# Transposes off TensorE: layer 2's input turned by VectorE and transfers, the RMS factor spread through DRAM, bias rows added on VectorE

## The chip, the core and the metric

The kernel runs on one core of one Trainium2 chip. Five engines work side by side, each through its own list of instructions in order: TensorE (PE in the profile; PEld is its loading of weights), VectorE (DVE), ScalarE (ACT), GpSimd (POOL) and SyncE (SP), which here only issues transfers (DMA). They meet through semaphores. The metric is the device time of one execution in microseconds; the median of three executions of the kernel before is 2365.2 us (2365.17 to 2367.01).

## The reference

32 graphs of 512 nodes with 256 features each go through four graph layers. Everything is float32. Cut to what matters (weights and small constants left out):

```python
def _layernorm(x):                      # over the last axis
    return (x - mean(x)) / sqrt(var(x) + 1e-5)

# layer 0
h = (1 + eps) * x + adj @ x
x = _layernorm(x + (relu(h @ W1 + b1) @ W2 + b2))                  # 256 -> 512 -> 256
# layer 1
h = adj @ (x @ W.T + b)
x = _layernorm(x + where(h > 0, h, alpha * h))
# layer 2
h = layer_norm(x, gamma, beta)
x = _layernorm(x + (x + relu((adj @ h) @ W_rel + b_rel + h @ W_root)))
# layer 3
h = (epsilon * x + adj @ x) @ W1 + b1                              # 256 -> 1024
h = silu(h * rsqrt(mean(h * h) + 1e-6) * rms_weight)               # RMS over the 1024
x = _layernorm(x + (h @ W2 + b2))                                  # 1024 -> 256
```

## The kernel before

A graph's features lie in a tile `room` of 128 partitions by 1024 floats: 128 nodes of each of four chunks, 256 features per chunk. Matrix products are done by a scheme with seven block products for a 2x2 split where eight are usual (`seven`, `left_sums`, `right_sums`); VectorE makes the sums of blocks that this needs, and adds results from PSUM. A product of 256 columns or of 128 is one matmul; in the trace each appears twice, as two passes.

No engine's order is written out by hand. Each step (`plan.do`, `plan.move`) is recorded as an `Op` with the engines that can do it and an estimated duration. `Plan.order` then runs through time and at each point gives the engine that is free first the operation with the lowest rank, where the rank grows with the number of the graph (`RULES`: period, pace, last, near). Up to `FLIGHT` = 4 graphs are in work at once, limited by 36 rooms, 12 small tiles (`few`) and the 8 banks of PSUM. Transfers are all issued by SP, in order, at most 8 at a time; the planner counts 0.45 us per issue and a fixed part before and after the data. It also keeps GpSimd's sums and VectorE's sums of two SBUF operands apart in time (`port`). All instructions pass through one helper, so almost every row of the profile has the line L266 (transfers: L280); tiles tell them apart.

Five places matter for what follows.

- `layer2` (L935 to L953). The product `h @ W_root` needs `h` with features on partitions. L938 to L943 turn it: for each of two feature blocks four transposes on TensorE (`flip`, a matmul with the identity `ident`) fill one bank, and one `copy` brings the bank to `hT`. `dense_sums` (L950) then makes VectorE's sums of `hT` and the aggregate `aT`, and `dense_add` multiplies.
- `layer3` (L955 to L990). `squares` sums the squares of the 1024 features, `column_sums` (L793) reduces over partitions with a transposing reduction and small sums, `inv_sqrt` has GpSimd raise to the power -0.5 with the result on 128 partitions, and L975 to L977 spread the 512 factors over all partitions with four flips into one bank `pr`. L981 multiplies the hidden features by `pr` on VectorE.
- `plus_row` (L874) adds the bias row of layers 0 and 3 to the residual, as four sums of 256 columns on GpSimd each time, eight per graph.
- `Adjacency` (L634). The adjacency arrives in four transfers of 256 KB. Layers 0 and 3 need it with a multiple of the identity added, layers 1 and 2 without. `sums` saves the four diagonal blocks in a room by transfers within SBUF (`carry`, L659 to L665), `with_loops` adds, `restore` (L667) carries them back.
- the order of layers per graph: `layer0`, `layer1`, `layer2`, `layer3`, with the output transfer at the end of `layer3` (L990).

```python
        for j in range(DC):
            ps = bank(N)
            for c in range(NC):
                flip(ps[:, c * P : (c + 1) * P], h[:, c, j * P : (j + 1) * P])
            copy(hT.chunk(j), ps)
```

Of the kernel before, what the change touches and what calls it, by code (L numbers as in the profile page):

```python
# [10 lines left out]
F32 = mybir.dt.float32  # L11
# [3 lines left out]
P = 128  # L15
# [11 lines left out]


def in_psum(x):
    return isinstance(x, Part) and x.room.pool.psum  # L30
# [35 lines left out]
def gpsimd_time(n):  # L66
    return 0.15 + n * 0.0024, 0.05


def power_time(n):  # L70
    return 0.37 + n * 0.158, 0.04
# [4 lines left out]
ISSUE, ADVANCE, AFTER, LANES = 0.45, 1.5, 0.35, 8  # L76
# [18 lines left out]
RULES = [(50, 2, last, near) for last in (12, 20) for near in (0, 0.5, 1)]  # L95


class Pool:


    def __init__(self, tiles, grain, spare, psum):
        self.tiles, self.grain, self.spare, self.psum = tiles, grain, spare, psum
        self.clear()

    def clear(self):
        self.rooms = [None] * len(self.tiles)

    def free(self):

        return sorted(  # L110
            (0.0 if r is None else r.until, i)
            for i, r in enumerate(self.rooms)
            if r is None or not r.left
        )


class Room:


    def __init__(self, pool):  # L120
        self.pool = pool
        self.uses = 0
        self.clear()

    def clear(self):
        self.index = None
        self.left = self.uses
        self.until = 0.0


class Part:
# [34 lines left out]
    def place(self):  # L166
        v = self.room.pool.tiles[self.room.index]
        for step in self.steps:
            v = step(v)
        return v  # L170
# [3 lines left out]
class Op:  # L174

    graph: int
    rank: tuple
    ways: dict  # L180
    port: set
    yields: bool
    kbytes: float
    rooms: list = field(default_factory=list)
# [6 lines left out]
class Plan:  # L191
# [10 lines left out]
    def grains(self, x):  # L202
        part = isinstance(x, Part)
# [4 lines left out]
        for step, n in dims[:-1]:  # L208
            starts = [s + step * i for s in starts for i in range(n)] if step else starts
        step, n = dims[-1]  # L210
        return {
            (key, g)
            for s in starts
            for g in range(s // grain, (s + step * (n - 1)) // grain + 1)
        }

    def add(self, ways, out, ins, ordered=None, port=(), kbytes=0):
        me = len(self.ops)
        op = Op(self.graph, (self.graph, me), ways, port, "scalar" in ways, kbytes)
        self.ops.append(op)  # L220
        before, results = set(), set()
        writes = self.grains(out) if out is not None else set()
# [22 lines left out]
    def do(self, out, *ways, ordered=None, scrap=None):  # L245
# [3 lines left out]
        port = set()  # L249
        for e, method, _, args, kw in ways:  # L250
            tiles = [x for x in (*args, *kw.values()) if isinstance(x, (bass.AP, Part))]
            ins += tiles
            if e == "gpsimd" and kw.get("op") != ALU.pow or e == "vector" and not (
                method.startswith("bn_") or any(in_psum(x) for x in tiles)
            ):
                port.add(e)

        def issue(engine, method, args, kw):
# [14 lines left out]
            out, ins, ordered, port,  # L273
        )

    def move(self, out, src, kbytes, inward=True):


        def issue():
            self.nc.sync.dma_start(*(x.place() if isinstance(x, Part) else x for x in (out, src)))  # L280

        self.add(
            {"sync": ((ISSUE, ADVANCE + wire_time(kbytes) + AFTER), issue)},
            out if inward else None, [src] if isinstance(src, Part) else [], kbytes=kbytes,
        )
# [31 lines left out]
    def order(self, period, pace, last, near):  # L317
# [15 lines left out]
        oldest, port, wire, lanes = 0, 0.0, 0.0, [0.0] * LANES  # L333
        can_start = {i for i, n in enumerate(behind) if not n}
        done = []
        while can_start:
# [4 lines left out]
            def rooms_free(op):  # L341

                count = {}
                for r in op.rooms:
                    if r.index is None:
                        count[r.pool] = count.get(r.pool, 0) + 1
                at = 0.0
                for pool, n in count.items():
                    if pool not in room_at:
                        room_at[pool] = pool.free()  # L350
                    n += pool.spare[min(op.graph - oldest, len(pool.spare) - 1)]
                    if op.graph - oldest >= self.flight or n > len(room_at[pool]):
                        return None
                    at = max(at, room_at[pool][n - 1][0])
# [3 lines left out]
            for i in can_start:  # L358
# [4 lines left out]
                if op.kbytes:  # L363
                    wait = max(wait, lanes[0])
                at = {
                    e: max(free[e], wait, ready[i][e], port if e in op.port else 0.0)
                    for e in op.ways
                }
                way = min(at, key=lambda e: at[e] + sum(op.ways[e][0]) + (YIELD if op.yields and e == "vector" else 0.0))
# [11 lines left out]
            if op.kbytes:  # L381
                wire = max(wire, t + ADVANCE) + wire_time(op.kbytes)
                end = wire + AFTER
                lanes = [*lanes[1:], end]
            if engine in op.port:
                port = end
            for r in op.rooms:
                if r.index is None:
                    r.index = r.pool.free()[0][1]
                    r.pool.rooms[r.index] = r  # L390
# [16 lines left out]
def tile_gnn_stack(ctx: ExitStack, tc: tile.TileContext, a: dict, out: bass.AP):  # L407
# [36 lines left out]
    FLIGHT, ROOMS, SMALL = 4, 36, 12  # L444
# [3 lines left out]
    psum = ctx.enter_context(tc.tile_pool(name="psum", bufs=1, space=bass.MemoryType.PSUM))  # L448
    plan = Plan(nc, FLIGHT)

    def pool(kind, name, n, size, grain, spare):
        return Pool(
            [kind.tile([P, size], F32, tag=f"{name}{i}", name=f"{name}{i}") for i in range(n)],
            grain, spare, kind is psum,
# [3 lines left out]
    rooms = pool(work, "room", ROOMS, NC * D, P, (0, 4, 6, 8))  # L458
# [5 lines left out]

    def gpsimd(method, n, *args, **kw):
        return "gpsimd", method, gpsimd_time(n), args, kw
# [22 lines left out]
    def both(method, o, x, y, engines):  # L489
        plan.do(o, *(e(method, span(o), x, y) for e in engines))  # L490

    def add(o, x, y, *engines):
        both("tensor_add", o, x, y, engines or (vector,))

    def sub(o, x, y, *engines):
# [590 lines left out]
```

## Time and profile before

| | |
|---|---|
| median of three executions | 2365.2 us |
| the profiled execution | 2366.0 us |
| its span (first to last instruction) | 2364.2 us |
| granted TensorE clock, mean | 0.997 |
| TensorE matmuls with `ident`, from `room` (layer 2) | 256, 273 ns each |
| the same from `few` (the RMS factor) | 128, 274 ns each |
| GpSimd bias rows, 128x256 | 256, 194.6 us busy, 769 ns each |
| GpSimd powers, 128x4 and 128x8 | 160, 212.5 us busy |
| VectorE sums of two SBUF operands, 128x512 | 672, 464.2 us busy, 696 ns each |
| VectorE sums of SBUF and PSUM, 128x512 (`room<-room,ps`) | 256, 170.5 us busy, 679 ns each |
| transfers within SBUF, 128 KB | 252, 2.2 us to landing |
| adjacency transfers, 256 KB | 128, 5.0 us to landing |
| output transfers, 512 KB | 32, 3.0 us to landing |

The page that these come from is of one execution. Busy time is the time in which at least one instruction of an engine was under way; [...]two of them overlap, and the distance between two starts is shorter than the duration. A group's row names output and inputs, shape and count, then busy time, the mean duration, and the idle time of the engine just before. Transfers are listed with the time from issue to landing; what SP spends on the issue itself is a separate record.

### The profile page before, as it was taken

What the parts mean: (1) busy time and instruction counts of PE and PEld (TensorE: products, weight loads), DVE (VectorE), ACT (ScalarE), POOL (GpSimd) and SP (SyncE); (2) the same over time, 40 slices, a digit from 0 to 9 for tenths busy, and PEclk for the clock granted to TensorE, in tenths of its full rate; (3) what the DMA queues carried; (4) which work ended last, traced back from release to release, by engine and by line L of the source; (5) the groups of instructions that cost most, each with busy time, mean ns of one, the idle gap of its engine ahead of it and who ended that gap; (6) DMA issues with size and microseconds to landing.
All of it is one profiled execution on the core that took longest, in us unless ns stands there. A gap on an engine that the chain in (4) does not pass through costs nothing.

```text
span 2364.2 us, 40948 instructions
## 1 busy us (share of the span) xinstructions
PE 2330.0 (99%) x14362; PEld 2135.4 (90%) x14362; DVE 2138.4 (90%) x5485; ACT 1570.1 (66%) x3994; POOL 407.7 (17%) x422
## 2 busy tenths in 40 slices
PE   8999999999999999999999999999999999989997
PEld 7899989999999999999999999999999989978997
DVE  6899989999999999999999999999999999988997
ACT  3767666667666676766676666776666766565764
POOL 1112111111121121111111211111111112111111
PEclk9999999999999999999999999999999999999999
DMA  7001110111110111101111101111011111011000
GB/s 218 12 8 54 50 54 12 52 50 51 53 35 30 50 54 50 54 14 50 50 52 52 44 20 50 54 50 54 14 50 50 52 52 46 23 52 48 10 10 28
DMA packets 103487, 107.25 MB, mean 45 GB/s; under 512 B 10865, under 2 KB 78193, under 8 KB 103281
## 3 DMA queue, kind: packets, MB, share of 16 engines
q1 hardware_dynamic: 103280, 104.64, 14.5%
q8 instruction: 113, 1.85, 0.3%
q14 instruction: 94, 0.76, 0.1%
HBM read 54.80 MB, written 16.78 MB: 30 GB/s over the span
## 4 chain that ended last, share of the span: by engine, by line
PE 91%; DVE 4%; DMA 2%; ACT 1%; issue 1%; SPq 0%; POOL 0%; POOLq 0%; ACTq 0%; DVEq 0%
PE ps L266 91%; DVE room L266 3%; ACT room L266 1%; DVE few L266 1%; DMA room<-in_x_dram 1%; ACT scrap L266 1%; DMA room<-room 1%; SPq L280 0%; DMA L_gnn_eps<-in_L_gnn_eps_dram 0%; DMA room<-in_adj_dram 0%; POOL few L266 0%; ACT L266 0%; POOLq L1082 0%; DVE L_gnn_W L266 0%; DVE A L266 0%
## 5 line engine op out<-in xcount | busy, mean ns | idle before, releaser
L266 PE MATMUL ps<-room,room 128*128 128x256 f32 x3584 | 911.9, 380 | 9.8 <-DMA room<-in_x_dram 5.8
L266 DVE TENSOR_TENSOR room<-ps,room 128x256 f32<-128x256 f32 (+1 forms) x1344 | 629.6, 475 | 149.3 <-PE ps L266 122.6
L266 PEld LDWEIGHTS ps<-room,room 128*128 128x128 f32 x3584 | 650.1, 191 | 88.8 <-issue 7.1
L266 DVE TENSOR_TENSOR room<-room,room 128x512 f32<-128x512 f32 (+1 forms) x1120 | 640.6, 585 | 9.9 <-ACT room L266 3.1
L266 PE MATMUL ps<-L_gnn_W,room 128*128 128x128 f32 (+1 forms) x3584 | 622.7, 291 | 7.2 <-ACT room L266 4.9
L266 PEld LDWEIGHTS ps<-L_gnn_W,room 128*128 128x128 f32 x3584 | 525.3, 192 | 31.1 <-ACT room L266 7.2
L266 PE MATMUL ps<-A,room 128*128 128x128 f32 x3072 | 489.2, 276 | 1.8 <-ACT room L266 1.1
L266 PEld LDWEIGHTS ps<-A,room 128*128 128x128 f32 x3072 | 434.8, 192 | 15.8 <-ACT room L266 1.3
L266 PE MATMUL ps<-room,L_gnn_W 128*128 128x256 f32 x1536 | 424.6, 380 | 1.0 <-DVE room L266 0.9
L266 ACT ACTIVATE room<-ps,L_gnn_b_c 128x256 f32<-128x256 f32 x768 | 318.2, 472 | 157.2 <-PE ps L266 157.0
L266 POOL TENSOR_TENSOR few<-few,mhalf 128x4 f32<-128x4 f32 (+1 forms) x160 | 212.5, 1329 | 1211.0 <-DVE few L266 1208.5
L266 ACT ACTIVATE room<-ps 128x256 f32<-128x256 f32 (+1 forms) x546 | 215.0, 407 | 298.5 <-PE ps L266 294.7
L266 ACT ACTIVATE room<-room,few 128x256 f32<-128x256 f32 x624 | 341.0, 603 | 107.0 <-DVE few L266 103.7
L266 DVE TENSOR_TENSOR room<-room 128x256 f32<-128x256 f32 (+1 forms) x640 | 330.4, 518 | 18.0 <-DMA room<-in_adj_dram 5.7
L266 POOL TENSOR_TENSOR room<-room,L_gnn_b 128x256 f32<-128x256 f32 x256 | 194.6, 769 | 739.6 <-PE ps L266 519.0
L266 PE MATMUL ps<-room,A 128*128 128x256 f32 x1152 | 319.2, 380 | 3.0 <-ACT room L266 3.0
L266 PEld LDWEIGHTS ps<-room,L_gnn_W 128*128 128x128 f32 x1536 | 279.7, 191 | 33.1 <-DVE room L266 2.2
L266 ACT ACTIVATE room<-room 128x1024 f32<-128x1024 f32 (+2 forms) x260 | 245.8, 946 | 18.1 <-DVE room L266 16.5
L266 ACT ACTIVATE room<-room,L_gnn_rms_weight_c 128x512 f32<-128x512 f32 x256 | 179.7, 718 | 111.3 <-DVE room L266 108.2
L266 PEld LDWEIGHTS ps<-room,A 128*128 128x128 f32 x1152 | 206.5, 191 | 27.1 <-ACT room L266 4.2
L266 ACT ACTIVATE scrap<-room 128x256 f32<-128x256 f32 x384 | 157.2, 411 | 74.3 <-DVE room L266 63.1
L266 ACT ACTIVATE scrap<-room,few 128x256 f32<-128x256 f32 x384 | 190.7, 498 | 18.1 <-DVE few L266 16.3
(53 smaller groups left out, 1453.4 us busy)
## 6 DMA issues: line engine op xcount, KB each, us to landing
room<-in_adj_dram SPq DMA_DIRECT2D x128, 256.0 KB, 5.0
room<-room SPq DMA_DIRECT2D x252, 128.0 KB, 2.2
room<-in_x_dram SPq DMA_DIRECT2D x32, 512.0 KB, 6.0
out_dram<-room SPq DMA_DIRECT2D x32, 512.0 KB, 3.0
L_gnn_W<-in_L_gnn_W_dram SPq DMA_DIRECT2D x2, 1024.0 KB, 8.5
L_gnn_W<-in_L_gnn_W_dram SPq DMA_DIRECT2D x2, 512.0 KB, 8.1
L_gnn_b<-in_L_gnn_b_dram SPq DMA_DIRECT2D x3, 128.0 KB, 5.0
L_gnn_W_rel<-in_L_gnn_W_rel_dram SPq DMA_DIRECT2D x1, 256.0 KB, 7.2
```

The costliest lines, as they stand in the source:

```text
L266: getattr(getattr(self.nc, engine), method)(to, *(put(x) for x in args), **kw)
```

## The change

For all graphs but the first and the last (`alone()`), the twelve flips per graph are replaced. `turned` has VectorE transpose the 32x32 blocks of `h` (two instructions of 128x512 into a room `squares`), and 16 transfers of 32 partitions by 8 pieces of 32 floats (128 bytes) each put the blocks in their places in `hT`. `everywhere` gathers the RMS factors in a 32x32 square with four small copies, transposes it on VectorE, writes 16 rows of 128 bytes to a line in DRAM, and reads the line back to all 128 partitions; `pr` is then a tile in SBUF. The bias rows become two sums of 128x512 on VectorE each. The diagonal blocks are no longer kept in SBUF: two of them are read again from the input in DRAM (as four transfers of 64 KB), two are saved to DRAM and read back (graph 0 keeps the old way). `with_loops` adds in place.

The planner changes with it: five graphs in work, rooms that can be taken in halves (`short`), dependencies followed by groups of 32 partitions, no keeping apart of GpSimd and VectorE, other rules of rank, other estimates for the power (0.3 + 0.21 per column for 0.37 + 0.158) and for the time after a transfer (0.8 us for 0.35), other reserves of free rooms, 11 small tiles for 12. The order of all engines is thus new.

The core of the diff; bookkeeping of half rooms and renamed helpers are left out:

```diff
-    return 0.37 + n * 0.158, 0.04
+    return 0.3 + n * 0.21, 0.04
...
-ISSUE, ADVANCE, AFTER, LANES = 0.45, 1.5, 0.35, 8
+ISSUE, ADVANCE, AFTER, LANES = dict(sync=0.45, gpsimd=1.5), 1.5, 0.8, 8
...
-RULES = [(50, 2, last, near) for last in (12, 20) for near in (0, 0.5, 1)]
+RULES = [(p, c, last, near) for p, c in ((36, 2), (45, 2.5)) for last in (12, 20) for near in (0.25, 0.5)]
...
-    FLIGHT, ROOMS, SMALL = 4, 36, 12
+    FLIGHT, ROOMS, SMALL = 5, 36, 11
...
+    memory = ctx.enter_context(tc.tile_pool(name="memory", bufs=1, space=bass.MemoryType.DRAM))
     plan = Plan(nc, FLIGHT)
+    lines = cycle([memory.tile([N], F32, tag=f"line{i}", name=f"line{i}") for i in range(FLIGHT)])
+    diagonals = cycle(
+        [
+            memory.tile([P, 2, 2, P], F32, tag=f"diagonal{i}", name=f"diagonal{i}")
+            for i in range(FLIGHT)
+        ]
+    )
+    def alone():
+        return plan.graph in (0, B - 1)
...
-    rooms = pool(work, "room", ROOMS, NC * D, P, (0, 4, 6, 8))
+    rooms = pool(work, "room", ROOMS, NC * D, P, (0, 2, 4, 4))
...
-            kept = room(4, HC, P)
-            self.plain = [kept[:, i] for i in range(4)]
-            for d, o in zip(self.plain, self.loops):
-                if plan.graph:
-                    carry(d, o)
+            if plan.graph:
+                self.kept = next(diagonals)
+                for i in (2, 3):
+                    d = self.kept[:, i - 2]
+                    name = f"{self.kept.tensor.name}{i}"
+                    plan.move(d, self.loops[i], P * HC * P / 256, into=name)
+            else:
+                self.kept = room(4, HC, P)
+                for i in range(4):
+                    copy(self.kept[:, i], self.loops[i])
+        def restore(self):
+            for i in range(4):
+                if plan.graph == 0:
+                    carry(self.loops[i], self.kept[:, i])
+                elif i < 2:
+                    for k in range(HC):
+                        c = i * HC + k
+                        block = a["adj"][plan.graph][:, c, c * P : (c + 1) * P]
+                        plan.move(self.loops[i][:, k], block, P * P / 256)
                 else:
-                    copy(d, o)
-        def restore(self):
-            for d, o in zip(self.plain, self.loops):
-                carry(o, d)
+                    name = f"{self.kept.tensor.name}{i}"
+                    d = self.kept[:, i - 2]
+                    plan.move(self.loops[i], d, P * HC * P / 256, outof=[name])
         def with_loops(self, loop):
-            for d, o in zip(self.plain, self.loops):
-                add(o, d, loop.unsqueeze(1).to_broadcast(list(o.shape)), vector)
+            for o in self.loops:
+                loops = loop.unsqueeze(1).to_broadcast(list(o.shape))
+                add(o, o, loops)
...
+    def by_token(o, sums, *ops):
         for q in range(P // Q):
-            put(slice(q * Q, (q + 1) * Q), few[0:Q, q :: P // Q])
+            ts(o[q * Q : (q + 1) * Q], sums[:, q :: P // Q], *ops)
...
+    def turned(h):
+        hT = Wide(DC)
+        if alone():
+            for k in range(DC):
+                ps = bank(N)
+                for c in range(NC):
+                    flip(ps[:, c * P : (c + 1) * P], h[:, c, k * P : (k + 1) * P])
+                copy(hT.chunk(k), ps)
+        else:
+            squares = Wide(DC)
+            for k in range(DC):
+                o = squares.chunk(k)
+                plan.do(o, vector("transpose", N, h[:, :, k * P : (k + 1) * P]))
+            places = [slice(q * Q, (q + 1) * Q) for q in range(P // Q)]
+            to, of = (
+                x.pair(0).then(lambda v: v.rearrange("p k (c i) -> p (k c) i", i=P))
+                for x in (hT, squares)
+            )
+            for p in places:
+                for q in places:
+                    carry(to[p, :, q], of[q, :, p])
+        return hT
+    def everywhere(sums, ops):
+        few = small(2, NC)
+        ve, power = few[:, 0, :], few[:, 1, :]
+        by_token(ve, sums, *ops)
+        inv_sqrt(power, ve)
+        if alone():
+            o = bank(N)
+            for c in range(NC):
+                flip(o[:, c * P : (c + 1) * P], power[:, c : c + 1].spread(P, P))
+        else:
+            few = small(2, Q)
+            square, turned = few[0:Q, 0, :], few[0:Q, 1, :]
+            for q in range(P // Q):
+                ts(square[:, q : N // Q : P // Q], power[q * Q : (q + 1) * Q], 1.0, None, ALU.mult)
+            plan.do(turned, vector("transpose", Q, square))
+            o, line = short(N), next(lines)
+            name = line.tensor.name
+            plan.move(line.rearrange("(m i) -> m i", i=Q), turned[0 : N // Q], N / 256, into=name)
+            plan.move(o, line.partition_broadcast(P), P * N / 256, late=0.8, outof=[name])
+        return o
     def plus_row(x, r):
-        for c in range(NC):
-            add(x[:, c, :], x[:, c, :], r, gpsimd)
+        for h in range(2):
+            add(half(x, h), half(x, h), r.unsqueeze(1).to_broadcast([P, HC, D]))
...
-        hT = Wide(DC)
-        for j in range(DC):
-            ps = bank(N)
-            for c in range(NC):
-                flip(ps[:, c * P : (c + 1) * P], h[:, c, j * P : (j + 1) * P])
-            copy(hT.chunk(j), ps)
+        hT = turned(h)
...
-        few = small(2, NC)
-        ve, rstd = few[:, 0, :], few[:, 1, :]
-        column_sums(acc, lambda p, sums: ts(ve[p], sums, 1.0 / HID3, RMS_EPS, ALU.mult, ALU.add))
-        inv_sqrt(rstd, ve)
-        pr = bank(N)
-        for c in range(NC):
-            flip(pr[:, c * P : (c + 1) * P], rstd[:, c : c + 1].spread(P, P))
+        pr = everywhere(column_sums(acc), (1.0 / HID3, RMS_EPS, ALU.mult, ALU.add))
```

## The prediction

> **What bounds the kernel now.** I read the page's busy shares first, then the busy time by stretches of the span, then the groups by shape, and last single stretches of the timeline, to get start-to-start intervals rather than durations.
>
> ```profile
> span 2364.2 us, 40948 instructions
> PE 2330.0 (99%) x14362; PEld 2135.4 (90%) x14362; DVE 2138.4 (90%) x5485; ACT 1570.1 (66%) x3994; POOL 407.7 (17%) x422
> ...
> PE 91%; DVE 4%; DMA 2%; ACT 1%; issue 1%; SPq 0%; POOL 0%; POOLq 0%; ACTq 0%; DVEq 0%
> ```
>
> ```profile
> core 0: us, PE busy (x) PEld busy (x) DVE busy (x) ACT busy (x) POOL busy (x), PEclk, DMA share, GB/s
> 0.00:72.00 72.00, 60.98 (x302) 51.78 (x302) 53.42 (x144) 30.93 (x82) 9.16 (x16) 0.98 0.60 181
> 900.00:1100.00 200.00, 200.00 (x1265) 184.65 (x1264) 184.28 (x468) 139.36 (x355) 38.09 (x39) 1.00 0.16 48
> 2056.00:2182.00 126.00, 117.91 (x702) 104.50 (x700) 105.15 (x283) 74.62 (x205) 17.32 (x17) 1.00 0.15 45
> 2320.00:2364.20 44.20, 31.57 (x234) 29.84 (x232) 34.22 (x89) 18.81 (x33) 4.03 (x4) 0.90 0.09 36
> ```
>
> From about 150 to 2056 us TensorE has no gap; what it loses lies at the start, around 2100 us and in the last 44 us. Busy durations overlap, so I price by intervals:
>
> ```profile
> 72.76 0.27 PE L266 MATMUL ps<-ident,room 128*128 128x128 f32 x1
> 72.87 0.60 PE L266 MATMUL ps<-room,room 128*128 128x256 f32 x2
> ```
>
> ```profile
> 1005.53 0.68 DVE L266 TENSOR_TENSOR room<-room 128x512 f32<-128x512 f32 x1
> 1006.13 0.41 DVE L266 TENSOR_TENSOR room<-ps,room 128x256 f32<-128x256 f32 x1
> 1006.47 0.68 DVE L266 TENSOR_TENSOR room<-room,room 128x512 f32<-128x512 f32 x1
> ```
>
> A transpose on TensorE lasts 0.27 us and costs 0.11: the next matmul starts 0.11 later. VectorE spends 0.60 us on 512 columns and 0.34 on 256, though it is listed with 0.68 and 0.41. By such intervals TensorE's list sums to 2308 us (3392 matmuls of 256 columns at 0.431, 3584 of 128 at 0.2225, 384 transposes at 0.11, the warm-up) and VectorE's to about 1995. So 56 us of the span are TensorE idle, nearly all at the ends, and VectorE has 14% to spare. The outputs leave every 72.1 us in the middle, which is TensorE's work per graph.
>
> ```profile
> L280 SPq DMA_DIRECT2D room<-room x252: 593/594/688, 13.7 to 2204.2; - x126
> L280 SPq DMA_DIRECT2D room<-in_adj_dram x128: 327/441/2332, 0.7 to 2175.2; - x128
> ```
>
> ```profile
> 0.74 1.81 SPq L280 DMA_DIRECT2D room<-in_adj_dram  x4
> 18.15 1.26 SPq L280 DMA_DIRECT2D room<-room  x2
> ```
>
> SP takes 0.46 us per transfer of 2 KB rows ((1.81-0.44)/3) and 0.66 for one of two 512 B pieces per partition (1.26-0.594). That difference carries the forecast.
>
> **What the Trainium skill says.** "TensorE: Matmul & The Clock Gate", Part 4: a TensorE transpose goes to PSUM and needs a copy behind it, some 275 ns in a kernel; the trace has 273 ns, but only 0.11 of it is TensorE's time. "VectorE: DVE Perf Modes", The three transpose paths: VectorE turns 32x32 blocks only, so something else must move the blocks; no run here shows that instruction, but the reduction with a transpose in it takes 705 ns for 512 columns, one element per cycle as any sum. "DMA: Bandwidth & Descriptors", Anatomy of one DMA: about 2 us of each transfer are fixed, mostly the receipt of the write; the trace has 2.2 us from issue to landing for 128 KB. The same page, Why small descriptors are slow: the penalty for small pieces is one of HBM, not of SBUF to SBUF; the packet records agree so far, with 28 ns for 512 B and 9 for 4 B.
>
> **The change part by part**, for the 30 graphs that are not the first or last.
>
> Flips. Eight per graph of `h` and four of the RMS factor leave TensorE: 360 x 0.11 = 39.6 us, 1.32 per graph. TensorE is gapless there, so this is the whole gain, if nothing new holds it.
>
> VectorE's load. Added: 60 transposes of 512 columns (0.60 to 0.65, by the row with a transpose in it), 37; 128 bias rows of 512 at 0.60, 77; 120 small copies and 30 small transposes at 0.085, 13; copies and scalings that the planner shifts between VectorE and ScalarE (-28 and +61 of 256), 11. Together 138: 2133 us against TensorE's 2268. From 86% it goes to 94%; still below TensorE, so not the bound by itself, but 4.5 us of slack per graph are left where there were 10. ScalarE loses 60 copies of 512 columns, GpSimd 195 us of sums; neither was on the path. That no GpSimd sum shares VectorE's SBUF access any more is worth nothing: sums of two SBUF operands take 696 ns, those with PSUM 679 to 685.
>
> The burst of 16. Both transposes done, SP issues 16 transfers of 32 KB; the first VectorE reading of `hT` waits for the last. In the order of after, what stands between the start of the second transpose and that reading is 10.5 us of VectorE work, and beside it 10.6 us of TensorE work, in every graph of the middle. The chain needs 0.7 (transpose) + 0.2 (hand to SP) + 15 issues + 2.0 to 2.2 (landing) + 0.1. With 0.46 per issue that is 10.0: hidden. With 0.66 it is 12.9 to 13.1: VectorE stands 2.4 us. Behind the standing instruction are the sums of other graphs; counting both queues onward from there, TensorE first runs out of VectorE's results after 0.6 us of lateness in one graph and after 1.1 in the next (the order repeats every two graphs). So at 0.66 TensorE loses 1.3 to 1.8 per graph, all of the gain; at 0.46 nothing. The new transfers have 256 pieces like the slow row and a quarter of its bytes. I take 0.60: chain 12.1, late by 1.5, loss 0.4 and 0.9, mean 0.65. Times 28 graphs, 18 us.
>
> The RMS row. The small transpose, a 2 KB write to DRAM, a 256 KB spread back. Bounds: 2.2 + 3.0 by the rows of SBUF copies and outputs, up to 3.0 + 5.0 by the output and adjacency rows (the latter queue four deep). Cover in the order: 6.9 to 7.3 us of TensorE work, and 0.8 more before TensorE feels it. I take 0; the upper end costs up to 0.3 per graph, 8 us. In before the chain ended in four flips that TensorE waited for only 1.9 us in all.
>
> Loads. The adjacency's landing had 28 us of cover; after it has 6.1 to 7.0 from the first of four issues. In before the fourth landed 7.2 us after the output transfer issued ahead of it; after gives 6.5 and 7.4. Late by at most 0.7, which is about the slack behind it: 0, with 0.2 per graph as the upper end. SP has 1003 transfers for 463; about 550 us of issuing in 2350, but in order, so a burst delays what stands behind it by up to 10 us. The diagonals saved to DRAM land with 3 us of cover against 2.6 measured for such a copy: 0. Their restoration has 10 us or more.
>
> Ends. First and last graph keep their flips. Five graphs in flight for four fill and drain differently; TensorE idles 56 us there now. Unknown sign; by the windows of start and end not over 10 either way, and I add 2.
>
> Sum against the profiled execution, 2366.0 (span 2364.2 plus 1.8): -39.6 + 18 + 2 = 2346.4; it lies 0.8 above the median, so 2346.
>
> **Rivals.**
> All hidden: issue at 0.46 or an early landing. For it: nothing but 0.2 us per issue separates it; against: the row of 594 ns hardly varies. -39.6 + 2: 2328, or 2323 with better ends.
> Nothing gained: issue at 0.65, loss 1.2 to 1.3 per graph: 2364.
> Slower: the same burst, longer. If 32-partition transfers cost SP 0.75, or land after 3 us as output rows do, the reading is 3.5 us late, TensorE loses 2.65 per graph, 1.33 more than it gains: about +37, 2402. It decides from the point where the chain exceeds 12.8 us (10.6 + 0.85 + 1.33). For it: 16 issues multiply every 0.05 us to 0.75; against: the packet records.
> VectorE as the bound: at 94% its waits no longer fit between its work, in the ends most: -40 + 60, 2386. Against: 2133 is still 135 below TensorE.
> That the change doesn't do what it says: no; the order of after has the 60 transposes, the 480 transfers and 24 flips.
>
> **How the numbers follow.** Forecast (2336 to 2357) 0.36; all hidden 0.22; nothing gained 0.13; slower by the burst 0.23; VectorE or the ends 0.06. The first two and a little of the third are faster: 0.60. A difference under 0.2%, about 4.7 us, is no change here: most of the third, 0.10. Slower 0.30. For 8 in 10 the range goes from 2322 to 2392, since the lower bound of the work is near 2323 and half of the slower case must be in.
>
> **What would show it.** Transposes of 512 columns at 690 to 710 ns on VectorE; TensorE's instructions down by 360; outputs every 70.8 us (hidden), 71.4 (forecast), 72.1 or more (nothing or slower). SP's line for the 16: its duration says which bound holds. A new wait of VectorE for those transfers of 1 to 2 us per graph, and waits of TensorE for VectorE that before hadn't. If VectorE waits for the RMS row or the adjacency instead, or TensorE is gapless and the ends grew, the mechanism is wrong.

## The result and the profile after

The changed kernel takes 2464.1 us (median of 4 runs, 2463.6 to 2465.2) against 2365.8 for the kernel before: ratio 1.0416, 95% interval 1.0397 to 1.0434. The forecast was 2346, the range ended at 2392. The profiled execution took 2464.4 us with a span of 2462.6; the granted clock was 0.998, before it was 0.997.

The page of the kernel after, shares first and then the chain that ended last:

```profile
span 2462.6 us, 40871 instructions
PE 2359.8 (96%) x14002; PEld 2093.6 (85%) x14002; DVE 2213.9 (90%) x5867; ACT 1512.0 (61%) x3901; POOL 247.3 (10%) x166
...
DVE 49%; PE 16%; SPq 11%; ACT 10%; DMA 7%; issue 4%; POOL 4%; DVEq 0%; POOLq 0%; ACTq 0%
```

TensorE has the 360 instructions less that were to go. Of the chain, 16% runs through it (91% before) and 49% through VectorE, with SP's issues, ScalarE, transfers and GpSimd between. The outputs leave every 76.2 us in the middle; before it was 72.1. So each graph costs 4.1 us more, where 1.3 less was the most to be had. The stretch from 600 to 1400 us holds ten and a half graphs. First the busy time of the engines in two stretches, in us out of the stretch's length in the second column:

```profile
core 0: us, PE busy (x) PEld busy (x) DVE busy (x) ACT busy (x) POOL busy (x), PEclk, DMA share, GB/s
...
900.00:1100.00 200.00, 193.21 (x1125) 170.56 (x1125) 181.77 (x483) 127.34 (x331) 21.95 (x13) 1.00 0.17 44
...
600.00:1400.00 800.00, 770.94 (x4555) 681.85 (x4554) 720.97 (x1911) 498.69 (x1287) 85.48 (x52) 1.00 0.18 48
```

The kernel before from 600 to 1400 us:

```profile
600.00:1400.00 800.00, 800.00 (x4963) 736.58 (x4962) 736.94 (x1890) 541.88 (x1380) 141.54 (x143) 1.00 0.15 44
```

TensorE was busy for all of the 800 us and is for 770.94 now. VectorE's waits from 600 to 1400 us (what waited for what: us in total, times, longest):

```profile
DVE room L284 <- ACT room L284: 22.4, 10, 2.3
DVE few L284 <- POOL few L284: 21.0, 16, 1.5
DVE room L284 <- DMA room<-room: 15.0, 10, 2.3
DVE room L284 <- PE ps L284: 8.6, 20, 0.9
DVE room L284 <- DMA room<-in_adj_dram: 7.0, 5, 2.7
```

and in the kernel before:

```profile
DVE room L266 <- PE ps L266: 39.3, 56, 1.7
DVE room L266 <- ACT room L266: 7.2, 22, 0.5
DVE few L266 <- ACT scrap L266: 5.2, 11, 0.5
DVE room L266 <- DMA room<-room: 0.4, 1, 0.4
```

There VectorE waits 52 us, 39.3 of them for TensorE: harmless, since TensorE has no gap. Now 65 of 74 us are for others: ScalarE, GpSimd, the burst of sixteen transfers, the adjacency. VectorE issues in order, so they add up: 68.7 us of work (721/800 of 76.2) and some 7 us of waits make the period. TensorE now stands behind both: in the same 800 us its weight loads wait 42.1 us for VectorE and 21.6 for ScalarE.

Two of these waits from close by, in the timeline of the kernel after (start, length, what; in brackets the idle time before it and what ended it). The first is GpSimd's power in layer 1's norm:

```profile
1003.30 0.22 DVE L284 TENSOR_SCALAR few<-few 128x4 f32<-128x4 f32 x2
1003.44 0.41 DVE L284 TENSOR_TENSOR room<-ps,room 128x256 f32<-128x256 f32 x1
1003.69 3.80 POOL L284 TENSOR_TENSOR few<-few,mhalf 128x8 f32<-128x8 f32 x1 [17.52 <-ACT room L284]
1003.77 1.87 DVE L284 TENSOR_TENSOR room<-room,room 128x512 f32<-128x512 f32 x3
1005.58 0.41 DVE L284 TENSOR_TENSOR room<-room 128x256 f32<-128x256 f32 x1
1007.52 0.23 DVE L284 TENSOR_TENSOR few<-few 128x4 f32<-128x4 f32 x2 [1.54 <-POOL few L284]
1007.67 0.42 DVE L284 TENSOR_TENSOR room<-room,room 128x256 f32<-128x256 f32 x1
1007.72 2.08 ACT L284 ACTIVATE room<-room,few 128x256 f32<-128x256 f32 x4 [1.96 <-DVE few L284]
```

In the kernel before, the same power stood beside small operations and sums from PSUM:

```profile
907.46 0.56 DVE L266 TENSOR_TENSOR few<-few 32x16 f32<-32x16 f32 x3
907.57 1.64 POOL L266 TENSOR_TENSOR few<-few,mhalf 128x8 f32<-128x8 f32 x1 [3.68 <-DVE few L266]
908.06 0.16 DVE L266 TENSOR_SCALAR few<-few 32x4 f32<-32x4 f32 x1
908.59 0.69 DVE L266 TENSOR_TENSOR room<-ps,room 128x512 f32<-128x512 f32 x1 [0.38 <-PE ps L266]
```

It took 1.64 us there and takes 3.80 here, where VectorE begins a run of sums with two SBUF operands just after it; all eleven powers of this shape between 600 and 1400 us agree with the one shown. VectorE then stands 1.54 us for it, and ScalarE 1.96 behind VectorE. The second is the burst. SP's sixteen issues in the same timeline:

```profile
1012.17 10.41 SPq L299 DMA_DIRECT2D room<-room  x16
```

and VectorE's operations at their end, with its stand for the last landing:

```profile
1020.86 0.41 DVE L284 TENSOR_TENSOR room<-ps,room 128x256 f32<-128x256 f32 x1
1021.20 0.67 DVE L284 TENSOR_SCALAR few<-few 32x4 f32<-32x4 f32 x4
1021.90 0.18 DVE L284 BATCH_NORM_AGGREGATE few<-few 128x2 f32<-128x6 f32 x1
1022.00 0.66 DVE L284 TENSOR_TENSOR room<-ps,room 128x512 f32<-128x512 f32 x1
1024.73 0.69 DVE L284 TENSOR_TENSOR room<-room 128x512 f32<-128x512 f32 x1 [2.08 <-DMA room<-room]
```

The issues follow each other at 0.65 us (10.41/16), and VectorE stands 2.08 us. From the start of the second transpose (1011.4) to the reading (1024.7) the chain took 13.3 us.

### The profile page after: what moved, and what is told of

Its sections match the earlier page's. It is cut to its first block, busy times and chain, and to the rows that moved or that the text cites. A ratio compares the mean times of both kernels' runs of the same rounds, so it can differ in the third digit from the quotient of the medians.

```text
span 2462.6 us, 40871 instructions
## 1 busy us (share of the span) xinstructions
PE 2359.8 (96%) x14002; PEld 2093.6 (85%) x14002; DVE 2213.9 (90%) x5867; ACT 1512.0 (61%) x3901; POOL 247.3 (10%) x166
## 4 chain that ended last, share of the span: by engine, by line
DVE 49%; PE 16%; SPq 11%; ACT 10%; DMA 7%; issue 4%; POOL 4%; DVEq 0%; POOLq 0%; ACTq 0%
DVE room L284 44%; PE ps L284 16%; SPq L299 11%; ACT room L284 7%; DVE few L284 5%; POOL few L284 4%; DMA room<-in_adj_dram 3%; ACT scrap L284 3%; DMA room<-room 2%; DMA diagonal<-room 1%; DMA room<-in_x_dram 0%; DMA L_gnn_eps<-in_L_gnn_eps_dram 0%; DMA L_gnn_b<-in_L_gnn_b_dram 0%; DVEq L284 0%; DVE A L284 0%
## 5 line engine op out<-in xcount | busy, mean ns | idle before, releaser
L284 PE MATMUL ps<-room,room 128*128 128x256 f32 x3584 | 949.5, 384 | 24.3 <-ACT room L284 15.2
L284 DVE TENSOR_TENSOR room<-room,room 128x512 f32<-128x512 f32 (+1 forms) x1360 | 774.3, 588 | 73.5 <-ACT room L284 55.5
L284 PEld LDWEIGHTS ps<-room,room 128*128 128x128 f32 x3584 | 622.9, 191 | 120.8 <-ACT room L284 39.8
L284 DVE TENSOR_TENSOR room<-ps,room 128x256 f32<-128x256 f32 (+1 forms) x1344 | 604.1, 468 | 43.1 <-PE ps L284 37.6
L284 PEld LDWEIGHTS ps<-L_gnn_W,room 128*128 128x128 f32 x3584 | 553.7, 191 | 87.1 <-DVE room L284 32.0
L284 PEld LDWEIGHTS ps<-A,room 128*128 128x128 f32 x3072 | 459.1, 191 | 63.4 <-DVE room L284 27.4
L284 POOL TENSOR_TENSOR few<-few,mhalf 128x4 f32<-128x4 f32 (+1 forms) x160 | 246.6, 1542 | 2209.5 <-DVE few L284 1794.3
L284 ACT ACTIVATE room<-room,few 128x256 f32<-128x256 f32 x563 | 301.9, 590 | 131.5 <-DVE few L284 131.3
L284 DVE TENSOR_TENSOR room<-room 128x256 f32<-128x256 f32 (+1 forms) x640 | 308.2, 492 | 56.3 <-DMA room<-room 48.9
L284 ACT ACTIVATE room<-ps 128x256 f32<-128x256 f32 x514 | 187.4, 373 | 64.7 <-PE ps L284 63.8
L284 DVE TENSOR_SCALAR few<-few 32x4 f32<-32x4 f32 (+2 forms) x792 | 117.5, 156 | 9.9 <-ACT scrap L284 5.0
```

Source lines behind the costliest of these rows:

```text
L284: getattr(getattr(self.nc, engine), method)(to, *(put(x) for x in args), **kw)
```

## Experiments

The theories at the start: A, VectorE's work and its stands in order add up; B, the burst alone is the loss; C, the held power alone. Beside each of them the kernel before took 2364 to 2366 us on the same chip. The times are of single executions unless a ratio is given; twenty executions of one kernel (three_true) spread over 10 us.

### Taking parts of the change back

**undo_turned.** In `turned`, so that flips are used in every graph and not in the first and last alone:

```
-        if alone():
+        if True:
             for k in range(DC):
```

> Layer 2's input is transposed by TensorE flips in every graph again; the RMS factors, powers, bias rows and the planner stay as changed. Theory A (VectorE binds: its work of about 66.7 us a graph plus the waits it stands through in order, about 8 us): the two transposes (1.4 us) and the stall of the burst (2.1 us) leave VectorE, up to 1.2 us of bank copies may come to it, so 2.3 to 3.5 us a graph over 28 graphs: 2365 to 2400 us, with GpSimd's 128x8 power still near 3.8 us and VectorE still waiting for it. Theory B (the burst alone is the loss): 2366 us or less, as before. Theory C (the held power alone is the loss): 2440 to 2464 us.

2399.2 us, 65 less. Not B, not C: A, at the upper end of its range, but not wholly for its reason. A had VectorE still waiting for GpSimd's power; from 600 to 1400 us that wait fell from 21.0 to 3.0 us as well, with the power at 2.95 us instead of 3.80.

**undo_row.** The same edit in `everywhere`.

> The RMS factors are spread by flips in every graph again; the rest stays as changed. Theory A: VectorE loses only five small instructions (about 0.8 us a graph), TensorE takes back 0.44 us a graph beside its idle time: 2440 to 2460 us. Theory B and C: no change beyond 10 us, 2454 to 2474 us.

2429.4 us, 35 less: outside both forecasts. More went than the five instructions: the order was planned anew, and VectorE's waits for GpSimd fell from 48.0 to 12.1 us in all. What one part is worth can't be read from undoing it where everything is planned again.

**undo_both.** Both edits.

> Both transposes by flips in every graph again; powers on 128 partitions, bias rows on VectorE, diagonals through DRAM and the new planner stay. Theory A: VectorE's work falls to about 64 us and its waits lose the burst's 2.1 us; with the remaining 5 to 6 us of waits it comes to 69 to 71 us a graph against TensorE's 72.1, so 2364 to 2385 us, the lower end if TensorE binds again. Theory B: 2364 us, TensorE without a gap. Theory C: 2440 us or more.

2387.6 us, 3 above A's range and 23 above the kernel before, although neither transpose is there. So not even both together are the whole loss.

**before_bias.** In the kernel before:

```
-        for c in range(NC):
-            add(x[:, c, :], x[:, c, :], r, gpsimd)
+        for h in range(2):
+            add(half(x, h), half(x, h), r.unsqueeze(1).to_broadcast([P, HC, D]))
```

> The kernel before with one part of the change: the two bias rows of each graph are added by VectorE (four adds of 128x512, about 2.7 us of work a graph) in place of GpSimd. Theory D (in the kernel before, VectorE's idle time is real slack: 39 of its 52 us of waits between 600 and 1400 us are for TensorE, 3.6 us a graph): the added work, less about 1 us a graph that VectorE's own sums gain when no GpSimd sum shares their access, fits: 2358 to 2372 us, TensorE without a gap. Theory E (VectorE's waits cannot be filled, so each us of added work is a us of period): 1.7 to 2.7 us a graph, 2410 to 2445 us.

2374.5 us. The busy times from 600 to 1400 us:

```profile
600.00:1400.00 800.00, 799.84 (x4964) 735.10 (x4964) 759.98 (x1945) 534.99 (x1368) 69.87 (x55) 1.00 0.15 44
```

VectorE is at 95% of the stretch, more than in the kernel after (90%), and TensorE has next to no gap; the outputs leave every 72.2 us. So E falls: VectorE's load by itself is not what makes the kernel after slow. D had the mechanism, and its range ended 2.5 us too low: of the 10 us over the kernel before, 2 lie ahead of the first output and 5 in the last seven graphs.

**short_power.** GpSimd's power becomes a product with zero, so the kernel leaves out the norms' scales. The operation, and its constant:

```
-    nc.vector.memset(mhalf, -0.5)
+    nc.vector.memset(mhalf, 0.0)
...
-            o, ("gpsimd", "tensor_tensor", power_time(n), (x, mhalf[0:p, 0:n]), dict(op=ALU.pow))
+            o, ("gpsimd", "tensor_tensor", power_time(n), (x, mhalf[0:p, 0:n]), dict(op=ALU.mult))
```

> GpSimd's powers are replaced by products with zero of the same shapes in the same order, so the norms' scales are not computed; each engine's list of instructions is otherwise the same. Theory A: VectorE's waits for GpSimd (1.54 + 0.82 us in a graph) and part of ScalarE's behind them go, 1.8 to 2.8 us a graph over 30 graphs: 2380 to 2410 us. Theory B: 2455 us or more, since the burst is untouched. Theory C: 2330 to 2370 us. If the product is held beside VectorE's sums as the power is, it too takes over 2 us where it meets them, and the time moves less than 20 us.

2432.1 us: 32 less, in none of the ranges. A had 54 to 84 less and C more; B had at most 9, so the burst isn't all; and that a held product would move less than 20 us failed too. GpSimd in its timeline:

```profile
964.48 0.20 POOL L284 TENSOR_TENSOR few<-few,mhalf 128x4 f32<-128x4 f32 x1 [2.47 <-DVE few L284]
991.27 2.36 POOL L284 TENSOR_TENSOR few<-few,mhalf 128x8 f32<-128x8 f32 x1 [18.33 <-ACT room L284]
```

A product lasts 0.20 us, and 2.36 where it meets VectorE's run of sums. That is 2.16 more, as 3.80 is 2.16 more than the power's 1.64. The hold is thus a wait of GpSimd's, the same for both operations, and it is as long as VectorE's run: where a run went on for 1.02, 1.45, 1.63, 2.29 or 2.65 us from the start of a power of 128x8 (undo_row, undo_turned, both_true, the kernel after, undo_row again), the power was longer by 0.89, 1.32, 1.49, 2.16 and 2.52. The run is 32 us faster with the hold still there, since the operations themselves are shorter, by 1.44 us for 128x8 and 0.81 for 128x4. VectorE no longer waits for GpSimd (0.6 us in all against 48.0), but its waits for ScalarE (58.1 us) and the burst (48.4) stay as they were (58.7 and 48.9). So ScalarE's lateness does not come from the power, as A had it in part.

### Correcting the planner's figures

The order is worked out from cost figures in the kernel. Three of them differ from the trace: 0.45 us for an issue (0.65 for a block transfer), 1.98 us for a power of 128x8 (3.80 when held), and 0.064 us for VectorE's scalars on 32 partitions. In the burst shown above four of these take 0.67 us, one every 0.17, while two scalars of 128x4 take 0.22. Theory F: the order is wrong, not the work. Theory G: VectorE has nothing else ready at those points, so the waits stay or others replace them. The edits touch only figures; the instructions stay, and only their order and the choice between VectorE and ScalarE for a few can move.

**issue_true** and **power_true**, one figure each:

```
-            {engine: ((ISSUE[engine], ADVANCE + late + wire_time(kbytes) + AFTER), issue)},
+            {engine: ((0.65 if kbytes == 32 else ISSUE[engine], ADVANCE + late + wire_time(kbytes) + AFTER), issue)},
```

```
-    return 0.3 + n * 0.21, 0.04
+    return 3.8 if n == 8 else 0.3 + n * 0.21, 0.04
```

> The changed kernel with one planner figure corrected: 0.65 us for the issue of a 32 KB block transfer; the power stays at the planner's 1.98. Theory F1 (the burst's wrong figure gives most of the 87 us that both figures gave back): 2380 to 2405 us, VectorE's wait for the burst gone and its wait for GpSimd still 1.5 us a graph or more. Theory F2 (the power's wrong figure gives most): 2435 to 2460 us.

> The changed kernel with the other figure corrected alone: 3.8 us for a power of 128x8; the burst's issues stay at the planner's 0.45. Theory F1: 2430 to 2455 us, VectorE's wait for the burst still about 2 us a graph. Theory F2: 2380 to 2410 us. If each figure gives about half, both runs lie between 2410 and 2430 us.

2416.5 us (48 less) and 2456.7 (7 less), nearer F1 than F2, though 11 and 2 above its ranges. From 600 to 1400 us, with the issue's figure alone VectorE's wait for the burst is gone, but that for GpSimd has grown from 21.0 to 29.4 us; with the power's alone GpSimd is no longer waited for, and the burst costs 21.4 us instead of 15.0. Each time the wait that was not corrected grew, and with the issue's figure the wait for the adjacency too, from 7.0 to 13.4 us.

**both_true**, both edits:

> The changed kernel with two of the planner's figures set to what the trace shows: 0.65 us instead of 0.45 for the issue of a 32 KB block transfer, 3.8 us instead of 1.98 for a power of 128x8; the instructions are the same, only their order may move. Theory F (the loss is order: VectorE is sent into waits that the planner did not know of): VectorE's waits for the burst and for GpSimd fall below 0.5 us each a graph, 2.5 to 4 us a graph return, 2360 to 2400 us. Theory G (VectorE has no other work ready then, so the waits stay or others take their place): 2440 us or more.

2376.8 us: 87 of the 98 us are back. One figure gives 48, the other 7, both 87: more than their sum. From 600 to 1400 us VectorE waits for neither the burst nor GpSimd; for ScalarE it waits 30.9 us, more than the 22.4 before the correction. G's 2440 us or more is out, though in part one wait did take the place of others.

**turned_true**, `undo_turned` with the power's figure:

> Layer 2's input by flips again, the RMS factors through DRAM, and the planner told 3.8 us for a power of 128x8. Theory F (only the order was wrong): TensorE's list is 0.44 us a graph shorter than before, no burst is there, VectorE has 1.4 us less to do than with the squares: 2345 to 2366 us. Theory G: as without the corrected figure, 2395 to 2400 us.

2423.9 us, worse than 2399.2 with the wrong figure, and 58 above F's range: neither theory had it. A single corrected figure gives another order, not surely a better one, while others are still wrong: here the powers of 128x4 took 1.62 us in the mean from 600 to 1400 us, against 1.01 when not held.

**small_true**, the third figure alone:

```
-        plan.do(o, vector("tensor_scalar", span(o), x, s1, s2, **kw))
+        way = vector("tensor_scalar", span(o), x, s1, s2, **kw)
+        if o.shape[0] == Q:
+            way = (*way[:2], (0.175, 0.085), *way[3:])
+        plan.do(o, way)
...
-            add(few[0:Q], few[0:Q], few[q * Q : (q + 1) * Q])
+            sides = few[0:Q], few[0:Q], few[q * Q : (q + 1) * Q]
+            plan.do(sides[0], ("vector", "tensor_add", (0.13, 0.085), sides[1:], {}))
```

> The changed kernel with a third planner figure corrected alone: VectorE's operations on 32 partitions, which the trace shows to follow one another at about 0.175 us (scalars of 32x4) and 0.13 us (adds of 32x16) instead of the planner's 0.064 and 0.077. Theory H (three wrong figures add up: each graph has 12 such scalars and 6 such adds, 1.3 to 1.6 us of VectorE work that the planner does not count): 30 to 70 us come back, 2395 to 2435 us, with the waits for the burst and for GpSimd still there. Theory I (the small operations do not matter; the power and the burst are all): 2455 us or more.

2419.8 us, 44 less, in H's range. From 600 to 1400 us VectorE's wait for the burst grew from 15.0 to 23.5 us, as H had it, but that for GpSimd is gone, against H, and that for ScalarE fell from 22.4 to 1.8.

**three_true**, the edits of issue_true and small_true, and

```
-    return 0.3 + n * 0.21, 0.04
+    return (2.7 if n == 8 else 1.2), 0.04
```

> The changed kernel with all three figures as the traces show them: 0.65 us for the issue of a block transfer, 2.7 us for a power of 128x8 and 1.2 us for one of 128x4 (the means with both figures corrected: 2.68 and 1.07 us), and 0.175 and 0.13 us for VectorE's operations on 32 partitions. Theory H: what both figures left (72.9 us a graph against TensorE's 70.8) goes too, 1 to 2 us a graph over 28 graphs: 2315 to 2350 us, faster than the kernel before. Theory I: 2370 to 2385 us, as with the two.

2360.9 us (ratio 0.9984, 0.9978 to 0.9991): 103 us less than the changed kernel, from figures alone, but 11 above the upper end of H's range and 9 below I's. The outputs leave every 72.2 us. The figures for the power are means of another run; from 600 to 1400 us the one of 128x8 then took 1.64 us and that of 128x4 1.17, so they are nearer to the trace than the old ones and not exact.

This shows that the loss lies in the order and not in the work. That it is the truth of the figures which makes the order good, and not merely another order, rests on a comparison: in the three runs with all the figures corrected that apply (this one, flips_three and twelve_three, below) TensorE is busy for 795.6 to 799.2 of the 800 us, and in the kernel after and the twelve other runs with the new planner for 770.9 to 794.1. No run gave the planner other figures that were equally far off, so how much an arbitrary new order moves the time is known only from side effects: 35 us less in undo_row, 25 more in turned_true.

### What is left, and a better version

**flips_three**: both transposes by flips, with the corrected figures for the power and the small operations.

> Both transposes by flips again, the rest of the change with the power's and the small operations' figures corrected (there is no burst). Theory H: TensorE's 72.1 us a graph bind without gaps; the ends are some 10 us shorter than before, as the same kernel with the planner's own figures showed: 2340 to 2368 us, so that the transposes themselves are worth 15 to 30 us against the run with all three. If the order and not the transposes makes the difference, it is within 5 us of that run.

2360.3 us (0.9980, 0.9972 to 0.9988), TensorE busy 799.2 of 800 us, 72.2 us a graph. That is within 1 us of three_true, as the second forecast had it. So the new transposes, with sixteen transfers, are worth nothing even in a good order.

**twelve**, **twelve_true** (with the first two figures) and **twelve_three** (with all three). The four blocks on the diagonal stay in their partitions, so ScalarE copies them and twelve transfers are left:

```
-                    carry(to[p, :, q], of[q, :, p])
+                    if p == q:
+                        act(to[p, :, p], of[p, :, p], AF.Copy)
+                    else:
+                        carry(to[p, :, q], of[q, :, p])
```

> The changed kernel with twelve transfers in the burst instead of sixteen: the four blocks on the diagonal are copied by ScalarE (128x32... four copies of 32 partitions x 256 elements a graph). The chain of SP's issues is four times 0.65 = 2.6 us shorter, more than VectorE's stand of 2.08 us for it. Theory A (burst, held power and late ScalarE add up): the burst's share goes, 1.5 to 2.5 us a graph over 28 graphs: 2394 to 2422 us. Theory B (the burst alone is the loss): 2330 to 2366 us. Theory C (the held power alone): 2455 us or more.

> Twelve transfers in the burst and the planner's two figures set to the measured ones, together. Theory F: no wait of VectorE for the burst or for GpSimd above 0.5 us a graph is left, and TensorE's 70.8 us a graph bind with gaps of about 1 us: 2335 to 2375 us. Theory G: within 10 us of the twelve transfers with the old figures.

> Twelve transfers in the burst (four copies by ScalarE) with all three figures corrected. With the burst known to the planner its length should hardly matter: within 10 us of the sixteen transfers. If the burst's chain of issues still holds VectorE, it is 15 to 40 us faster.

2424.1, 2382.2 and 2334.7 us. The first is 40 less than the changed kernel, 2 beyond A's range. The second is 7 above F's range and no better than sixteen transfers (2376.8), within the spread. The third has ratio 0.9870 (0.9855 to 0.9885) to the kernel before: the only version here over 1% faster, and 26 us below sixteen transfers with the same figures, in the range of its second forecast. From 600 to 1400 us, its busy times:

```profile
600.00:1400.00 800.00, 798.04 (x4893) 729.78 (x4892) 767.55 (x2024) 553.90 (x1420) 94.10 (x55) 1.00 0.19 50
```

all of VectorE's waits in it:

```profile
DVE room L284 <- PE ps L284: 24.7, 44, 1.3
```

and those in three_true:

```profile
DVE room L284 <- PE ps L284: 18.2, 22, 1.3
DVE room L284 <- DMA room<-in_adj_dram: 6.4, 10, 1.4
DVE few L284 <- POOL few L284: 6.3, 6, 1.1
DVE room L284 <- DMA room<-in_x_dram: 3.3, 6, 1.0
DVE room L284 <- ACT room L284: 2.8, 5, 0.6
```

With twelve, VectorE waits for TensorE alone, at 96% busy, and TensorE binds again, every 71.4 us. With sixteen it isn't the burst that it waits for, though the second forecast rested on that, but TensorE, GpSimd, ScalarE and loads, the latter in the same queue of SP's as the burst; that four issues fewer set the loads free is argued from the two lists and not shown by a run of its own; both orders are new throughout.

**split_13**: the 128x8 power as two of 128x4 (1.3 us each in the planner), with the issue's figure.

> The changed kernel with the power of 128x8 in two of 128x4 (1.3 us each for the planner, which is between the 1.01 and 1.38 us that the trace shows) and 0.65 us for the issue of a block transfer. If the long stand of a power beside VectorE's sums is what counts, two short ones end 1.3 us sooner for the first half, and the time is below that with both figures corrected: 2350 to 2376 us. If VectorE's sums hold each of the two again (2.2 us more each), it is no better: 2376 to 2410 us.

2406.7 us, worse than one long power with both figures true. The short ones take 1.37 us in the mean instead of 1.01, so they too are held; the figure of the small operations was still wrong there.

## Why the prediction was wrong

**Flips: 1.32 us per graph.** The size was right, but not all of it was to be had. Between flips_three and twelve_three, both with TensorE 99.8% busy or more, lie 72.2 - 71.4 = 0.8 us a graph and 26 us in all, not 39.6. The traces say where the rest went. From 600 to 1400 us a flip is followed after 0.109 us in the kernel before and in flips_three, and matmuls of 256 and 128 columns at the same medians, 0.216 and 0.112 us, in all three. What differs are gaps: intervals over 0.02 us longer than these medians add up to 0.6 us a graph in twelve_three, 0.3 in flips_three and nothing in the kernel before. TensorE's weight loads wait 10.8 us in that stretch of twelve_three against 3.6 in flips_three.

**VectorE's load: "4.5 us of slack per graph are left".** This step failed, in part by its size and above all by its use. In size, the added work was right: the median intervals from one start to the next, times the counts from 600 to 1400 us, sum to 63.8 us a graph before and 68.2 after, and 4.4 more is what was forecast (138/32 = 4.3). The base was low, 62.3 (1995/32) for 63.8, because some 14 small operations a graph on 32 partitions took 0.19 to 0.20 us each in the kernel before, and not the 0.085 that the prediction gives small operations. The Trainium skill has a model for such a cost ("VectorE: DVE Perf Modes", Two Vector instructions with no wait between them): an instruction whose operands start in another group of 32 partitions than the last ones is held until every earlier one has finished. The trace agrees: in the kernel after, scalars of 32x4 follow each other at 0.17 us, which is all of the 0.16 us that one lasts and no overlap. The slack was 71.2 - 68.7 = 2.5 us (TensorE's busy time per graph in twelve_three, VectorE's in the kernel after), not 4.5. In use, the prediction spent the same slack several times, pricing each stall alone, although the stalls come in one in-order queue: 65 us of waits for engines and transfers other than TensorE in ten and a half graphs, 6.2 a graph. And it took for granted that the order was good. It put an issue at 0.60 us and read the cover out of an order worked out from 0.45; what else an order from short figures does wrong it did not ask. With those figures corrected the same work loses none of the 98 us.

**What was left out: GpSimd's power.** An item with no price in the prediction: it names no power, and says that shared access to SBUF was now worth nothing. The Trainium skill ("GPSIMD Engine Reference", 8. Key points) states that GpSimd shares its SBUF interfaces with VectorE and contends with instructions of two SBUF inputs; the trace agrees and shows the size, 2.16 us, the length of the run. In the kernel before, the power of 128x8 ran beside small operations and sums from PSUM. No rule did that: the old planner's `port` leaves out powers too, so it was the order alone. What the hold by itself costs no run shows; a shorter operation under it gave 32 us (short_power), and the power's figure alone 7 (power_true).

**The burst: 0.60 us per issue, late 1.5, 0.65 per graph.** The place and the mechanism were right, the term was too small: 0.65 per issue, 2.8 us from the last issue (1012.17 + 15 x 0.65) to the reading, late by 2.08. By the prediction's own steps (late by 0.6 and 1.1 free) that is 1.2 per graph, 34 us instead of 18; with its planner figure corrected 48 came back. The landing was as forecast, 2.0 us in the median, and packets of 128 bytes took 13 ns where those of 512 took 27. The slower rival was to decide from a chain of 12.8 us, and at 13.3 it gives 2366 + 0.5 x 28 = 2380: right in sign, and 84 us short, because it let the lateness fall on a queue that, in its account, was late for nothing else.

**Rivals.** The nearest in mechanism was VectorE as the bound, at 0.06 and 2386. But before_bias and twelve_three carry 95 and 96% with TensorE busy for 799.8 and 798.0 of 800 us. It is the order that can't carry it: its figures are short by 16 x 0.2 = 3.2 us in SP's chain of the burst, by 1.8 in the power and by 12 x 0.11 + 6 x 0.05 = 1.6 in the small operations. That is an estimate of 6.6 us a graph against 2.5 of slack, though the three lie on different engines. What no addition of this sort gives is how much of it surfaces: 76.2 - 71.2 = 5 us a graph did.

**Transposes, RMS row, diagonals, adjacency.** A transpose of 512 columns lasts 684 ns and adds 0.60: right. Row and diagonals at nothing: right, the waits for them are 0.2 and 1.1 us in the whole span. Adjacency: 7.0 us of VectorE's waits in 10.5 graphs, 0.7 a graph, the lateness named; it was put at nothing. **GpSimd's sums gone, worth nothing:** wrong, in the good direction. VectorE's sums of 128x256 within one room took 457 ns beside them, 418 in before_bias and 415 in undo_both, from 600 to 1400 us. **Ends.** They were put at +2 and not over 10 either way; 28 graphs at 4.1 us would be 115, and 98 were measured, so by this estimate the ends gave some 17 back.

## What to carry to other kernels

Where a kernel orders its instructions by cost figures, compare each figure that a change leans on with the trace, in the new place and shape, and set the sum of the errors against the slack of the in-order engine that must absorb them; a load of 96% was harmless where the order knew the costs. Correct such figures together: one alone moved the loss to the next wrong one. And try a burst of transfers with fewer of them: with all three figures corrected, four issues fewer made the difference between no gain and 1.3%, with two of them none.

## What was not expected of the hardware

- GpSimd's small operation waits for the whole of VectorE's uninterrupted run of two-SBUF sums: 0.20 us became 2.36, 1.64 became 3.80, and 4.15 in undo_row. In the kernel after, the power begins 0.08 us before the run and is held all the same. In both_true, powers of 128x4 that began 0.24 us or more before the end of a sum from PSUM were not held (1.01 us). The boundary is open: one that began at 744.86 us in the kernel after, beside a small sum and 0.08 us ahead of a sum of two SBUF operands, took 1.01 us too.
- VectorE at 96% of a stretch of 800 us left TensorE nearly without a gap (798 of 800).
- Scalars of 32x4 whose start partitions change follow at 0.17 us, those of 128x4 at 0.07.
- A transfer of 32 KB in pieces of 128 bytes costs SP 0.65 us to issue and lands after 2.0 us.
